# Four-part KANs on four column strips, and bank-emptying copies given out at the head of a turn

## The chip, the cores and the metric

The kernel runs on one core of a Trainium2 chip. A core has five engines that run side by side, each with a queue of its own that it works through in order: TensorE (PE in the profile; PEld is its loading of weights), VectorE (DVE), ScalarE (ACT), GpSimd (POOL) and SyncE (SP), which here only issues DMAs. TensorE writes its results into PSUM, eight banks of 128 x 512 float32, and ScalarE and VectorE copy them out. The metric is the time on the device in microseconds, lower is better: the median over several executions.

## The reference, cut to what matters

Sixteen sequences of 512 tokens with 128 channels pass through six residual steps, each on a layer-normed input:

```python
x = x + 0.5 * kan(ln(x))                 # L0_ffn
x = x + attention(ln(x))                 # L0_attn: 16 query heads and 4 key heads of 8, causal, rotary
x = x + 0.5 * kan(ln(x))                 # L0_ffn again, same weights
x = x + 0.5 * experts(ln(x))             # L1_ffn: 8 experts, each takes its top 128 tokens
x = x + recurrence(ln(x))                # L1_attn: a gated linear scan along the tokens
x = x + 0.5 * experts(ln(x))             # L1_ffn again

def kan(x, Win, bin_, W1, b1, W2, b2, Wout, bout):      # M = 64, INNER = 16
    s = jnp.einsum('btd,dm->btm', x, Win) + bin_
    h = jax.nn.relu(s[..., None] * W1 + b1)             # 64 x 16 = 1024 hidden values a token
    g = jnp.einsum('btmh,mh->btm', h, W2) + b2
    return jnp.einsum('btm,md->btd', g, Wout) + bout
```

A KAN is run 32 times, twice for each sequence. Its hidden layer has 1024 values for each token, which are eight tiles of 128 partitions x 512 tokens; what matters here is how the eight tiles are summed back to 64 channels.

## The kernel before, in words

The kernel has a front part (constants, first KANs), an attention part of 16 blocks, and an expert part.

**Blocks and turns.** Block b (0 to 15) has 44 turns. A turn gives out one step of `weights` for sequence b (the scores transposed into a bank `ps_st`, L622, then the exponential on ScalarE, L625, then the causal mask on GpSimd, L627) and one step of `maxima` for sequence b + 1 (the scores into a bank `ps_sc`, L564, and their row maximum on VectorE, L569 and L574). Both kinds of banks exist twice, so TensorE can be two turns ahead of ScalarE and of VectorE. Blocks -1 and 15 do only one of the two.

**Side work.** Everything else is written as Python generators that are advanced by one step in `turn()` (L1046): first those in `urgent`, then those in `sides`. The order in which a generator emits its instructions is the order in the engines' queues (TensorE, ScalarE, VectorE, GpSimd are ordered by hand; DMA issues on SyncE follow the program). Side work that needs a PSUM bank takes one of two shared banks with `bank()` (L222) and gives it back with `freed()` (L231). Typical is `turned` (L285): in one turn four transposes into a bank; in the next turn, after that turn's exponential and maximum have been emitted, the copy out of the bank. In blocks 0 to 15 the side work is paced: `need()` holds a step back when what it wants of an engine (in rough units) is over what is left of the turn's budget `MOST` (L197), and `take()` books work without waiting.

**A KAN** (`kan`, L299) norms and transposes x, multiplies by `win`, whose 64 columns stand in it twice, so that 128 partitions hold the 64 channels in two copies (L303), copies the result to `kan_s` (L307), and then in eight steps, paced to 15 turns, makes a hidden tile on ScalarE from `kan_s` with a scale and a bias for each partition (L329): a tile holds two of the 16 inner units of all 64 channels. After every second step two matmuls (L335) sum two hidden tiles into the bank `ps_kg`, the one into partitions 0 to 63, the other into 64 to 127; their weights `w2d` are 128 x 64, so the two stand on different column halves of the array. One copy (L340) and four matmuls with `wout` (L346) end it. `kan_held` lets one KAN at a time into this part.

**Attention's input** (`attn_in`, L375) makes queries and keys in float32 and cuts each into three bfloat16 parts in `parts` (L353): copy on ScalarE, subtract on GpSimd, copy on ScalarE, subtract on GpSimd. **Outputs** (`outputs`, L633) multiplies the weights with the values, four groups of heads on four column strips of 32 (L645), copies the bank (L651), transposes it (L656) and divides (L660, L661). The tail of `stage_out` runs a row's second KAN and its gate.

**The front part** issues the weights' DMAs on ScalarE's and SyncE's queues (L68, L123 to L157), and `prepare` (L466) makes the KAN's constants. **The expert part** (L1107) alternates one step of `experts` with one turn of side work (the recurrence, the routing, the transposes of gathered tokens).

Of the kernel before, what the change touches and what calls it, by code (L numbers as in the profile page):

```python
# [16 lines left out]
P = 128  # L17
S = 512
# [3 lines left out]
HALF = 8  # L22
# [22 lines left out]
def tile_macaron(  # L45
# [51 lines left out]
    with ExitStack() as ph:  # L97
# [5 lines left out]
        hp = ph.enter_context(tc.tile_pool(name="p1_h", bufs=4))  # L103
# [14 lines left out]
        win = cst.tile([D, 2, M], F32, name="win")  # L118
        binc = cst.tile([P, 1], F32, name="binc")
        kw1 = cst.tile([P, HALF], F32, name="kw1")  # L120
        kb1 = cst.tile([P, HALF], F32, name="kb1")
        kw2 = cst.tile([P, HALF], F32, name="kw2")
        nc.scalar.dma_start(out=win, in_=win_in.unsqueeze(1).to_broadcast([D, 2, M]))  # L123
        nc.scalar.dma_start(out=kw1, in_=kw1_in.rearrange("m (a h) -> a m h", a=2))
        nc.scalar.dma_start(out=binc, in_=bin_in.unsqueeze(0).to_broadcast([2, M]))
        nc.scalar.dma_start(out=kb1, in_=kb1_in.rearrange("m (a h) -> a m h", a=2))
        nc.scalar.dma_start(out=kw2, in_=kw2_in.rearrange("m (a h) -> a m h", a=2))
        kb2 = cst.tile([M, 1], F32, name="kb2")
        nc.scalar.dma_start(out=kb2, in_=kb2_in.unsqueeze(1))
        wout = cst.tile([P, D], F32, name="wout")  # L130
        nc.scalar.dma_start(out=wout, in_=wout_in.unsqueeze(0).to_broadcast([2, M, D]))
# [3 lines left out]
        rbias = cst.tile([P, HALF], F32, name="rbias")  # L135

        w2d = cst.tile([P, HALF, M], F32, name="w2d")
        eye2 = cst.tile([P, M], F32, name="eye2")
# [16 lines left out]
        nc.sync.dma_start(out=rope, in_=rope_in)  # L155
        for b in range(1, B):
            load(b)  # L157
# [75 lines left out]

        def together(*gs):

            got, live = [None] * len(gs), list(enumerate(gs))
            while live:
                left = []
                for i, g in live:
                    try:  # L240
                        next(g)
                        left.append((i, g))
                    except StopIteration as end:
                        got[i] = end.value
                live = left
                if live:
                    yield
            return got
# [36 lines left out]
        def turned(src, name, pool):  # L285
            ps = yield from bank([P, NT, P], F32, "ps_t", 0.55)
            for c in range(NT):
                nc.tensor.transpose(ps[:, c, :], src[:, c, :], ident)
            yield
            dst = pool.tile([P, S], F32, name=name)  # L290
            take(act=0.6)
            nc.scalar.copy(dst, ps.rearrange("p c q -> p (c q)"))
# [6 lines left out]
        def kan(b):  # L299

            _, xT = yield from norm(x[b])
            ps = yield from bank([P, S], F32, "ps_s", 0.9)
            nc.tensor.matmul(ps, lhsT=win.rearrange("d a m -> d (a m)"), rhs=xT, start=True, stop=True)  # L303
            yield
            sk = w2p.tile([P, S], F32, name="kan_s")
            take(act=0.6)
            nc.scalar.copy(sk, ps)  # L307
            freed()
            yield
            while kan_held[0]:  # L310
                yield
            kan_held[0] = 1
# [4 lines left out]
            for t in range(HALF + 1):  # L317
                while now[0] < begin + 15 * t // 8:
                    yield
                pair = t % 2 == 0 and t > 0  # L320
                work = {"act": 0.8} if t < HALF else {}
                if pair:
                    work["pe"] = 1.0
# [3 lines left out]
                if t < HALF:  # L327
                    h = hp.tile([P, S], F32, name="kan_h")
                    nc.scalar.activation(h, sk, AF.Relu, bias=rbias[:, t : t + 1], scale=kw1[:, t : t + 1])  # L329
                    hs.append(h)  # L330
                if t == 1:
                    nc.gpsimd.tensor_tensor(x[b], x[b], kcst.unsqueeze(1).to_broadcast([P, NT, D]), ALU.add)
                if pair:
                    for i in range(2):
                        nc.tensor.matmul(pg[i * M : (i + 1) * M, :], lhsT=w2d[:, t - 2 + i, :], rhs=hs[t - 2 + i],  # L335
                                         start=(t == 2), stop=(t == HALF))
                yield
            gT = hp.tile([P, S], F32, name="kan_h")
            take(act=0.6)
            nc.scalar.copy(gT, pg)  # L340
# [4 lines left out]
            for c in range(NT):  # L345
                nc.tensor.matmul(po[:, c, :], lhsT=gT[:, bass.ts(c, P)], rhs=wout, start=True, stop=True)  # L346
            yield
            take(dve=0.7)
            nc.vector.tensor_add(x[b], po, x[b])
# [3 lines left out]
        def parts(r, dst, copies, **work):  # L353
# [4 lines left out]
            yield from need(pool=1.15)  # L358
            nc.gpsimd.tensor_tensor(r, r, dst[:, 0, :], ALU.subtract)
            yield  # L360
            yield from need(**work)
            copies(dst[:, 1, :], r)
# [12 lines left out]
        def attn_in(b, st):  # L375
# [8 lines left out]
            nc.tensor.matmul(pa, lhsT=wq.rearrange("k h d -> k (h d)"), rhs=xT, start=True, stop=True)  # L384
            yield
            take(dve=0.7)
            nc.vector.tensor_mul(ta, pa, rope[:, 0, :])
            freed()
            pb = yield from bank([P, S], F32, "ps_pb", 0.9)
            nc.tensor.matmul(pb, lhsT=wqr.rearrange("k h d -> k (h d)"), rhs=xT, start=True, stop=True)  # L390
            yield
            take(dve=0.7)
            nc.vector.tensor_mul(tb, pb, rope[:, 1, :])
            freed()
            pk = yield from bank([2 * KR, S], F32, "ps_pk", 0.9)
            nc.tensor.matmul(pk, lhsT=wk.rearrange("k w h d -> k (w h d)"), rhs=xT, start=True, stop=True)
            yield
# [3 lines left out]
            nc.vector.tensor_mul(ka, pk[0:KR, :], rope[0:KR, 0, :])  # L401
            pv = yield from bank([P, NT, KR], F32, "ps_v", 0.9)
            for c in range(NT):
                nc.tensor.matmul(pv[:, c, :], lhsT=xT[:, bass.ts(c, P)], rhs=wv, start=True, stop=True)
            yield
            take(dve=0.7)
            nc.vector.tensor_mul(kb, pk[KR : 2 * KR, :], rope[KR : 2 * KR, 1, :])
# [3 lines left out]
            yield  # L411

            take(dve=0.3)
# [3 lines left out]
            nc.vector.tensor_copy(va[:, :, :, 0:HD], pv.rearrange("p c (r d) -> p c r d", d=HD))  # L417
# [3 lines left out]
            def keys():  # L421
                yield from need(pool=1.25)
                nc.gpsimd.tensor_tensor(ka, ka, kb, ALU.add)
                yield
# [27 lines left out]
        def center_win():  # L452
            psc = yield from bank([P, 2 * M], F32, "ps_kc0")
            centered(psc, win.rearrange("d a m -> d (a m)"))
            freed()
# [10 lines left out]
        def prepare():  # L466

            nc.vector.scalar_tensor_tensor(rbias, in0=kw1, scalar=binc, in1=kb1, op0=ALU.mult, op1=ALU.add)
            nc.vector.tensor_add(eye2, ident[:, 0:M], ident[:, M:P])
            for u in range(HALF):  # L470
                nc.vector.tensor_scalar(w2d[:, u, :], eye2, kw2[:, u : u + 1], 0.5, ALU.mult, ALU.mult)
# [5 lines left out]
            nc.tensor.matmul(psc, lhsT=kb2, rhs=wout[0:M, :], start=True, stop=True)  # L477
# [100 lines left out]
        def max_rows(b, half, maxs):  # L578
# [15 lines left out]
            for c in range(NT):  # L594
                nc.tensor.transpose(pm[:, c, :], ms[:, c, :, :].rearrange("p i h -> p (i h)"), identb)
            yield
            mr = w2p.tile([3 * H2, S], BF16, name="mr")
            take(dve=0.4)
            nc.vector.tensor_copy(mr, pm.rearrange("p c q -> p (c q)"))
# [33 lines left out]
        def outputs(b, st, r):  # L633
# [4 lines left out]
            for c in range(NT):  # L638
# [5 lines left out]
                for g in range(NG):  # L644
                    nc.tensor.matmul(po[32 * g : 32 * g + 32, c * P : S], lhsT=va[:, c, r, :],  # L645
                                     rhs=pt[:, g, OFF[c] : OFF[c] + n], start=(c == 0), stop=(c == NT - 1))
                if c in (0, NT - 1):
                    yield
            oT = w2p.tile([P, NT, P], F32, name="oT")
            yield from need(act=0.6)  # L650
            nc.scalar.copy(oT.rearrange("p c q -> p (c q)"), po)  # L651
# [3 lines left out]
            for c in range(NT):  # L655
                nc.tensor.transpose(pq[:, c, :, :].rearrange("p r w -> p (r w)"), oT[:, c, :], ident)  # L656
            yield
            rd = small.tile([P, NT, NG, 1], F32, name="rden")
            take(dve=0.55)
            nc.vector.reciprocal(rd, pq[:, :, :, HD : HD + 1])  # L660
            nc.vector.tensor_mul(y[:, :, r, :, :], pq[:, :, :, 0:HD], rd.to_broadcast([P, NT, NG, HD]))  # L661
# [4 lines left out]
        def stage_out(b, st):  # L666
# [4 lines left out]
            for c in range(NT):  # L671
                nc.tensor.matmul(po[:, c, :], lhsT=yT[:, bass.ts(c, P)], rhs=wo, start=True, stop=True)
            yield
            take(dve=0.7)
            nc.vector.tensor_add(x[b], po, x[b])
# [10 lines left out]
        def gated(k, b):  # L686
# [4 lines left out]
            for c in range(NT):  # L691
                nc.tensor.matmul(ps[:, c, :], lhsT=xT[:, bass.ts(c, P)], rhs=gateT, start=True, stop=True)
            yield
            take(dve=0.2)
            nc.vector.tensor_copy(scores[b // GB][:, :, b % GB, :], ps)
# [116 lines left out]
        def dispatch():  # L812
            while taken[0] < NR * B:
                yield
            for i in range(0, len(order), 2):
# [10 lines left out]
                for j in range(2):  # L826
                    nc.tensor.transpose(ps[:, j, :], xgs[i // E % 2][:, i % E + j, :], ident)
                yield
                copy = nc.vector.tensor_copy if i % 4 else nc.scalar.copy
                copy(xins[i // E % 2][:, i % E : i % E + 2, :], ps)  # L830
# [105 lines left out]
        def folded():  # L936


            tmp = w2p.tile([P, 2, M, 4], F32, name="wu", tag="kan_s")
# [41 lines left out]
        def recurrence(pair):  # L981
# [6 lines left out]
            for a in range(2):  # L988
                nc.tensor.matmul(pf[half[a], :], lhsT=wf, rhs=xTs[a], start=True, stop=True)
            yield  # L990
            fg = w2p.tile([P, S], F32, name="fg", tag="kan_s")
            nc.scalar.activation(fg, pf, AF.Tanh, scale=0.5)
# [5 lines left out]
            nc.tensor.matmul(pl, lhsT=wlam, rhs=fg, start=True, stop=True)  # L998
            yield
# [165 lines left out]
```

## Time and profile before

| | us |
|---|---|
| median of 3 executions | 1751.41 (1749.4 to 1756.8) |
| the profiled execution, its own time | 1746.91 |
| its span, first to last instruction | 1745.2 |
| TensorE busy in the span | 1636.9 (94%) |
| VectorE, ScalarE, GpSimd busy | 1107.3, 996.6, 977.6 |

The profile is one execution. A group row names line, engine, operation, the tiles written and read, the shape and the count, then the busy time in us, the mean ns of one, and the idle time of the engine before it. Ends of matmuls are modelled and overlap the next matmul's start, so that what a product costs TensorE is read from its start to the start of the next product in the timeline. The first score product of block 0 starts at 116.3 us, the blocks' first turns then at 161.7, 215.2, 276.5, 332.1, 387.6, 443.2, 498.8, 554.3, 609.9, 667.3, 721.5, 782.0, 841.5, 897.3 and 949.7, and the first expert product at 1003.0. Blocks 3 to 8 take 55.6 us each.

### The profile page before, as it was taken

What the parts mean: (1) busy time and instruction counts of PE and PEld (TensorE: products, weight loads), DVE (VectorE), ACT (ScalarE), POOL (GpSimd) and SP (SyncE); (2) the same over time, 40 slices, a digit from 0 to 9 for tenths busy, and PEclk for the clock granted to TensorE, in tenths of its full rate; (3) what the DMA queues carried; (4) which work ended last, traced back from release to release, by engine and by line L of the source; (5) the groups of instructions that cost most, each with busy time, mean ns of one, the idle gap of its engine ahead of it and who ended that gap; (6) DMA issues with size and microseconds to landing.
All of it is one profiled execution on the core that took longest, in us unless ns stands there. A gap on an engine that the chain in (4) does not pass through costs nothing. (4 is left out here: it accounts for less than half of the span.)

```text
span 1745.2 us, 35245 instructions
## 1 busy us (share of the span) xinstructions
PE 1636.9 (94%) x12879; PEld 1111.0 (64%) x12879; DVE 1107.3 (63%) x3604; ACT 996.6 (57%) x2000; POOL 977.6 (56%) x1453
## 2 busy tenths in 40 slices
PE   6788999999999999899899899999999999999997
PEld 2334444444444444444444389899988889989997
DVE  6677767777787788788876137643467444672222
ACT  3445667777777776677667654344443334444443
POOL 2524535545565455455534767567663777647773
PEclk9889999999999999999999899999998999999999
DMA  4211111011110111011122113233322233323342
GB/s 117 76 52 36 44 44 43 28 42 51 54 37 32 42 55 47 16 48 54 35 70 63 31 44 73 51 64 73 62 60 45 55 73 63 66 56 71 68 82 48
DMA packets 101753, 94.77 MB, mean 54 GB/s; under 512 B 11859, under 2 KB 90140, under 8 KB 101340
## 3 DMA queue, kind: packets, MB, share of 16 engines
q1 hardware_dynamic: 74512, 67.45, 12.5%
q0 software_dynamic: 26048, 24.93, 8.8%
q8 instruction: 101, 1.65, 0.4%
q14 instruction: 72, 0.59, 0.1%
q10 hardware_dynamic: 1020, 0.15, 0.0%
HBM read 58.93 MB, written 37.49 MB: 55 GB/s over the span
## 5 line engine op out<-in xcount | busy, mean ns | idle before, releaser
L625 ACT ACTIVATE pt<-ps_st 128x512 f32<-128x512 f32 (+1 forms) x704 | 386.9, 561 | 238.3 <-PE ps_st L622 232.9
L627 POOL TENSOR_SCALAR_AFFINE_SELECT pt<-pt 128x128 f32<-128x128 f32 (+2 forms) x704 | 247.0, 355 | 405.0 <-ACT pt L625 400.4
L569 DVE CUSTOM_DVE_ANT_0 below<-ps_sc,causal 128x512 bf16<-128x512 f32 (+1 forms) x512 | 316.5, 618 | 117.2 <-PE ps_sc L564 103.1
L881 ACT ACTIVATE mo<-ps_h 128x512 f32<-128x512 f32 x256 | 153.1, 598 | 262.2 <-PE ps_h L879 262.0
L805 POOL DMA_INDIRECT xg<-xnd,tokI x256 | 249.9, 976 | 80.5 <-issue 42.8
L879 PE MATMUL ps_h<-xin,mw 128*128 128x128 f32 x2048 | 281.1, 281 | 0.0
L894 PE MATMUL ps_y<-mw,mo 128*128 128x128 f32 x2048 | 274.7, 278 | 0.0
L564 PE MATMUL ps_sc<-kp,qp 72*128 72x512 bf16 (+3 forms) x1024 | 260.7, 307 | 10.6 <-DVE maxs L569 8.0
L622 PE MATMUL ps_st<-qp,kp 99*128 99x512 bf16 (+3 forms) x1024 | 259.8, 307 | 5.7 <-ACT pt L625 4.8
L879 PEld LDWEIGHTS ps_h<-xin,mw 128*128 128x128 f32 x2048 | 252.7, 194 | 6.3 <-issue 3.7
L926 POOL DMA_INDIRECT sum<-ye,tokI x124 | 201.3, 1624 | 97.7 <-ACT ye L897 31.2
L894 PEld LDWEIGHTS ps_y<-mw,mo 128*128 128x128 f32 x2048 | 251.7, 194 | 2.3 <-issue 1.0
L622 PEld LDWEIGHTS <-kp 99*128 99x128 bf16 x1024 | 94.2, 101 | 203.8 <-issue 185.4
L329 ACT ACTIVATE kan_h<-kan_s,rbias,kw 128x512 f32<-128x512 f32 x256 | 206.6, 814 | 7.1 <-PE ps_kg L335 6.9
L574 DVE TENSOR_REDUCE maxs<-ps_sc 128x2 f32<-128x512 f32 (+1 forms) x192 | 130.6, 685 | 70.5 <-PE ps_sc L564 69.3
L335 PE MATMUL ps_kg<-kan_h,w2d 128*64 128x512 f32 x512 | 164.7, 640 | 3.1 <-ACT kan_h L329 3.0
L645 PE MATMUL ps_av<-pt,va 128*32 128x512 f32 (+3 forms) x2048 | 166.8, 444 | 0.0
L564 PEld LDWEIGHTS <-qp 72*128 72x128 bf16 x1024 | 97.5, 100 | 55.6 <-issue 33.9
L900 DVE TENSOR_TENSOR mo<-mo 128x128 bf16<-128x128 f32 x132 | 38.3, 290 | 137.8 <-ACT mo L885 137.6
L912 PE MATMUL acc<-mo 128*128 128x128 bf16 x1584 | 113.0, 220 | 6.0 <-DVE mo L900 5.8
L912 PEld LDWEIGHTS <-mo 128*128 128x128 bf16 x1584 | 99.5, 99 | 23.8 <-issue 22.5
L645 PEld LDWEIGHTS ps_av<-pt,va 128*32 128x32 f32 x2048 | 53.6, 109 | 93.0 <-issue 49.7
(195 smaller groups left out, 2308.8 us busy)
## 6 DMA issues: line engine op xcount, KB each, us to landing
qp<-qs SPq DMA_DIRECT2D x64, 288.0 KB
xnd<-kan_x SPq DMA_DIRECT2D x32, 256.0 KB
sum<-x SPq DMA_DIRECT2D x31, 256.0 KB
qs<-qpart SPq DMA_DIRECT2D x48, 128.0 KB
kp<-ks SPq DMA_DIRECT2D x48, 96.0 KB
x<-in_L_attn_x_dram SPq DMA_DIRECT2D x16, 256.0 KB
mw<-in_L_ffn_w_dram SPq DMA_DIRECT2D x16, 256.0 KB
xg<-xnd,tokI POOLq DMA_INDIRECT x256, 2.5
```

Of the source, the lines that this page charges most:

```text
L329: nc.scalar.activation(h, sk, AF.Relu, bias=rbias[:, t : t + 1], scale=kw1[:, t : t + 1])
L564: nc.tensor.matmul(v[:, u, 0:n], lhsT=qp[r][0 : 9 * HD, g, bass.ts(c, P)], rhs=kp[0 : 9 * HD, r, 0:n], start=alone, stop=(u == len(gs) - 1 ...
L569: nc.vector.tensor_tensor_reduce(below[:, 0:n], v[:, 0, 0:n], causal[:, S - n : S], 1.0, LOWEST, ALU.add, ALU.max, accum_out=maxs[:, c, h ...
L622: nc.tensor.matmul(v[:, u, 0:n], lhsT=kp[ROWS, r, bass.ts(c, P)], rhs=qp[r][ROWS, g, c * P : S], start=True, stop=True)
L625: nc.scalar.activation(o, v[:, :, 0:n], AF.Exp, scale=HD ** -0.5)
L627: nc.gpsimd.affine_select(out=dg, in_=dg, compare_op=ALU.is_ge, fill=0.0, base=0, pattern=[[0, len(gs)], [1, P]], channel_multiplier=-1)
L645: nc.tensor.matmul(po[32 * g : 32 * g + 32, c * P : S], lhsT=va[:, c, r, :], rhs=pt[:, g, OFF[c] : OFF[c] + n], start=(c == 0), stop=(c == ...
L805: nc.gpsimd.indirect_dma_start(out=xgs[i // E % 2][:, i % E, :], out_offset=None, in_=xnd[b], in_offset=bass.IndirectOffsetOnAxis(ap=tokI[ ...
L879: nc.tensor.matmul(pst[:, f, :], lhsT=mw1[e][:, bass.ts(f, P)], rhs=xins[i // E % 2][:, i % E, :], start=True, stop=True)
L894: nc.tensor.matmul(py, lhsT=hs[u][:, f, :], rhs=mw2[e][:, f, :], start=(f == 0), stop=(f == NF - 1))
L912: nc.tensor.matmul(acc[:, c, :], lhsT=sels[u][:, bass.ts(c, P)], rhs=yes[u][:, w, :], start=(e == 0 and c == 0 and w == 0), stop=(e == las ...
L926: nc.gpsimd.indirect_dma_start(out=sums[k, b], out_offset=bass.IndirectOffsetOnAxis(ap=tokI[g][:, n : n + 1], axis=0), in_=ye[:, b % 2 * ( ...
```

## The change

- The KAN works in four parts instead of two copies. `win` holds each half of the 64 channels four times, and the product with it is made twice, once for each half (`ps_s`, then `kan_s0` and `kan_s1`). A hidden tile holds four inner units of 32 channels. The eight tiles are summed by two groups of four matmuls, each with 128 x 32 weights, each matmul on a column strip of its own (at steps 4 and 8, instead of pairs at steps 2, 4, 6 and 8). Hidden tiles have five buffers instead of four. The constants are laid out to match, with more and smaller DMAs, some of them moved from ScalarE's queue to SyncE's.
- Copies and other operations that empty a bank of side products are put on a list `later` when the product is given out, and `flush()` emits them at the head of the next turn, ahead of that turn's score products, exponential and maximum. Before, they came after these. The same call stands in the expert part ahead of the experts' step.
- In `parts`, the second bfloat16 part is made on GpSimd by a subtraction that writes bfloat16 (ScalarE copy before), so that the order is copy, subtract, subtract, subtract.
- The front runs 17 turns instead of 14 before the second sequence's input starts, the keys start two steps later, and `mr` has one buffer instead of two.

The diff, cut to its core (the other bank-emptying operations, L651 to L1023, are moved to `later` in the same way):

```diff
-HALF = 8
+MH = M // 2
+NI = 4
+NV = 4
...
+        win = cst.tile([D, 2, NI, MH], F32, name="win")
+        binc = cst.tile([P, 2], F32, name="binc")
+        kw1 = cst.tile([P, 2, NV], F32, name="kw1")
+        def inner(dst, src):
+            for half in range(2):
+                rows = src[half * MH : (half + 1) * MH, :]
+                nc.scalar.dma_start(out=dst[:, half, :], in_=rows.rearrange("m (i v) -> i m v", i=NI))
+        for half in range(2):
+            cols = win_in[:, half * MH : (half + 1) * MH]
+            nc.sync.dma_start(out=win[:, half, :, :], in_=cols.unsqueeze(1).to_broadcast([D, NI, MH]))
+        def out_weights():
+            for half in range(2):
+                rows = slice(half * M, half * M + MH)
+                nc.sync.dma_start(out=kb2[rows, :], in_=kb2_in[half * MH : (half + 1) * MH].unsqueeze(1))
+                nc.sync.dma_start(out=wout[half * M : (half + 1) * M, :],
+                                  in_=wout_in[half * MH : (half + 1) * MH, :].unsqueeze(0).to_broadcast([2, MH, D]))
...
         nc.sync.dma_start(out=rope, in_=rope_in)
+        out_weights()
         for b in range(1, B):
             load(b)
...
+        later = []
+        def flush():
+            for emit in later:
+                emit()
+            later.clear()
...
             for c in range(NT):
                 nc.tensor.transpose(ps[:, c, :], src[:, c, :], ident)
-            yield
             dst = pool.tile([P, S], F32, name=name)
+            later.append(lambda: nc.scalar.copy(dst, ps.rearrange("p c q -> p (c q)")))
+            yield
             take(act=0.6)
-            nc.scalar.copy(dst, ps.rearrange("p c q -> p (c q)"))
             freed()
...
-            ps = yield from bank([P, S], F32, "ps_s", 0.9)
-            nc.tensor.matmul(ps, lhsT=win.rearrange("d a m -> d (a m)"), rhs=xT, start=True, stop=True)
-            yield
-            sk = w2p.tile([P, S], F32, name="kan_s")
-            take(act=0.6)
-            nc.scalar.copy(sk, ps)
-            freed()
-            yield
-            while kan_held[0]:
-                yield
-            kan_held[0] = 1
+            sk = []
+            for half in range(2):
+                while half and kan_held[0]:
+                    yield
+                kan_held[0] |= half
+                ps = yield from bank([P, S], F32, "ps_s", 0.9)
+                nc.tensor.matmul(ps, lhsT=win[:, half, :, :].rearrange("d i m -> d (i m)"), rhs=xT,
+                                 start=True, stop=True)
+                sh = (w1p if half else w2p).tile([P, S], F32, name=f"kan_s{half}")
+                later.append(lambda sh=sh, ps=ps: nc.scalar.copy(sh, ps))
+                yield
+                take(act=0.6)
+                freed()
+                sk.append(sh)
+            yield
...
+            U = 2 * NV
+            for t in range(U + 1):
                 while now[0] < begin + 15 * t // 8:
                     yield
+                four = t in (U // 2, U)
+                work = {"act": 0.8} if t < U else {}
+                if four:
                     work["pe"] = 1.0
                 if t == 1:
                     work["pool"] = 1.25
                 yield from need(**work)
+                if four:
+                    for half, v, h in hs:
+                        o = half * M + v % 2 * MH
+                        nc.tensor.matmul(pg[o : o + MH, :], lhsT=w2d[:, half, v, :], rhs=h,
+                                         start=(t < U), stop=(t == U))
+                    hs = []
+                if t < U:
+                    half, v = t // 2 % 2, t // 4 * 2 + t % 2
                     h = hp.tile([P, S], F32, name="kan_h")
+                    nc.scalar.activation(h, sk[half], AF.Relu, bias=rbias[:, half, v : v + 1],
+                                         scale=kw1[:, half, v : v + 1])
+                    hs.append((half, v, h))
...
             copies(dst[:, 0, :], r)
             yield
             yield from need(pool=1.15)
+            nc.gpsimd.tensor_tensor(dst[:, 1, :], r, dst[:, 0, :], ALU.subtract)
+            yield
+            yield from need(pool=1.15)
             nc.gpsimd.tensor_tensor(r, r, dst[:, 0, :], ALU.subtract)
-            yield
-            yield from need(**work)
-            copies(dst[:, 1, :], r)
             yield
             yield from need(pool=1.3)
             nc.gpsimd.tensor_tensor(dst[:, 2, :], r, dst[:, 1, :], ALU.subtract)
...
-            yield from need(act=0.6)
-            nc.scalar.copy(oT.rearrange("p c q -> p (c q)"), po)
+                    later.append(lambda: nc.scalar.copy(oT.rearrange("p c q -> p (c q)"), po))
...
         def turn():
+            flush()
             urgent[:] = [g for g in urgent if step(g)]
             sides[:] = [g for g in sides if step(g)]
             refill()
...
             for i in range(TURNS):
+                flush()
                 step(wts)
                 step(mxs)
...
+        working = True
+        while working or sides:
+            flush()
+            working = step(main)
             turn()
```

## The prediction

> **What bounds the kernel now.** Read first: the page's busy shares, then engines by stretch (stretch, length, then busy time and count of PE, PEld, DVE, ACT, POOL, clock, DMA).
>
> ```profile
> PE 1636.9 (94%) x12879; PEld 1111.0 (64%) x12879; DVE 1107.3 (63%) x3604; ACT 996.6 (57%) x2000; POOL 977.6 (56%) x1453
> 443.20:498.80 55.60, 54.72 (x397) 26.90 (x397) 42.98 (x144) 42.03 (x77) 30.09 (x63) 1.00 0.13 43
> 721.50:782.00 60.50, 55.28 (x393) 27.59 (x392) 49.39 (x161) 41.38 (x76) 31.50 (x64) 0.97 0.12 40
> ```
>
> The second line is block 6, one of six alike: TensorE 98% busy, VectorE and ScalarE 76 to 77%. The third is a block with routing on VectorE (49.4 of 60.5). Busy alone proves little, as matmuls overlap; so next, TensorE's waits, first in blocks 4 to 8, then behind them:
>
> ```profile
> PE ps_s L303 <- ACT kan_xT L292: 3.6, 5, 0.7
> PE ps_o L672 <- ACT yT L292: 0.8, 5, 0.2
> ...
> PE ps_t L288 <- DVE y L661: 7.2, 5, 2.9
> PE ps_st L622 <- ACT pt L625: 3.0, 8, 0.5
> PE ps_ko L346 <- DVE rope_kb L407: 2.1, 1, 2.1
> ```
>
> Five blocks hold 4.4 us of waits. TensorE's stream sets the time there; later some waits on operations that empty side banks (L661, L407) come in. Then what a product costs, from TensorE's timeline of block 6 (start, length, engine and line), start to next start:
>
> ```profile
> 473.63 1.02 PE L303 MATMUL ps_s<-kan_xT,win 128*128 128x512 f32 x2
> 474.50 0.38 PE L622 MATMUL ps_st<-qp,kp 99*128 99x512 bf16 x1
> ...
> 481.20 2.02 PE L335 MATMUL ps_kg<-kan_h,w2d 128*64 128x512 f32 x4
> 483.15 0.39 PE L622 MATMUL ps_st<-qp,kp 99*128 99x256 bf16 x2
> ...
> 484.65 0.38 PE L564 MATMUL ps_sc<-kp,qp 72*128 72x512 bf16 x1
> 484.96 1.08 PE L335 MATMUL ps_kg<-kan_h,w2d 128*64 128x512 f32 x4
> 485.97 0.39 PE L622 MATMUL ps_st<-qp,kp 99*128 99x512 bf16 x1
> 486.20 0.38 PE L564 MATMUL ps_sc<-kp,qp 72*128 72x512 bf16 x1
> 486.51 1.06 PE L645 MATMUL ps_av<-pt,va 128*32 128x512 f32 x8
> 487.51 0.39 PE L622 MATMUL ps_st<-qp,kp 99*128 99x512 bf16 x1
> 487.73 0.38 PE L564 MATMUL ps_sc<-kp,qp 72*128 72x512 bf16 x1
> 487.95 0.38 PE L622 MATMUL ps_st<-qp,kp 99*128 99x512 bf16 x1
> ```
>
> The first product with `win` takes 0.87. A KAN pair takes 1.01 (484.96) when both hidden tiles are there, and 1.95 (481.20) when the second is late. Four strips of 128 x 32, each with its own 128x512 operand, take 1.00 (486.51): four matmuls for the price of two. A score product ahead of strips takes 0.31, elsewhere 0.22 (487.73): 0.09 for each entry.
>
> **The change, part by part.** The sum is against the profiled execution, 1746.91 us (span 1745.2 and 1.7 around it), 4.5 below the median of 1751.41.
>
> *Pairs to quads.* 26 KANs run in blocks 0 to 15. Their 104 pairs, added up in the timeline, hold TensorE 125.6 us, 4.83 a KAN; 4.05 of it would be four undisturbed pairs, 0.78 is lateness. After: two groups at 1.00, two entries fewer (-0.18), one product with `win` more (+0.87). That is 4.83 + 0.18 - 2.00 - 0.87 = 2.14 a KAN, 56 us; if all the lateness comes back elsewhere 1.36, 35 us. The lateness is ScalarE's backlog of hidden tiles. A group of four has its last tile given out two turns ahead, as a pair has, but meets it twice a KAN, not four times; on the other hand TensorE's turns without side products, 0.33 to 0.45 in the timeline, grow more frequent, and there the exponential (0.49 start to start) and a hidden tile (0.70) are what is waited for. I keep a third of 20: -42.
>
> The row of four strips decides this. The Trainium skill, TensorE: Matmul & The Clock Gate, Part 3, gives three column tiles side by side 2.38 times the speed of one, 0.79 for each. By that rule four would come to 3.2 times; with 0.97 for a matmul alone (half of the late pair) a group would take 3.9/3.2 = 1.2 us, an estimate, and 52 such groups would make the sum 11 us poorer. The trace does not agree: its group of the same shape took 1.00.
>
> *Routing blocks.* Blocks 9 to 13 have VectorE at 49.4 of 60.5. If TensorE's share falls by 4, VectorE's own work is 87% of the rest: some of the gain of these ten KANs (about 16) stays behind. From 0 to +15, near the low end as VectorE still has room: +5.
>
> *Second copy to `kan_s`.* 26 more copies on ScalarE (L307: 580 ns, 0.46 start to start), cover: ScalarE idles 13.6 us of block 6, two more copies take 1.2. In `parts` two casts a block leave it (L362, 617 ns), so its load stands. 0; without cover +12. The Trainium skill, TensorEngine Tiling, PSUM Bottleneck, warns that tiling doesn't speed up evacuation: by it this copy would count. ScalarE's 76% here lets it hide.
>
> *GpSimd's extra subtraction.* Two a block at 1.15 (the row of L359) on 30.1 of 55.6. Behind them on its queue stand the masks L627, whose readers are the value products two steps later. A row's input begins four blocks ahead and must be ready two blocks later, so a few turns more hold nobody: 0, up to +4. The `mr` copies with one buffer are half a block (28 us) apart, their DMAs keep their place: 0.
>
> *`flush`.* The copy moves ahead of the next turn's score evacuations on ScalarE and VectorE. Its product stands on TensorE ahead of those scores, so it is ready first and holds nobody idle. What stands behind it (exponential, maximum) comes 0.46 to 0.68 later; with two score banks TensorE feels that only over three light turns in a row. The bank comes free by one exponential or maximum sooner: of the waits shown (L661, L407, kan_xT; 13 us in blocks 4 to 15) I take a quarter: -3, from -8 to +10.
>
> *Front and tail.* Five KANs run before block 0 (0 to 116 us), latency-bound: one more product and copy each (0.87 + 0.58), three turns more. On SyncE's queue four issues stand newly ahead of `wq` and four ahead of the 15 loads of x, at the 0.4 to 0.5 that its issues take; they push the second row's load from 5.3 to about 9 us, and its norm starts at 22.5. ScalarE issues fewer. Against it stand the shorter sums: +2, from -4 to +8. In the experts the same TensorE stream is untouched, and gaps at `ps_x` and `acc` (about 10 us) can move either way: -1, from -4 to +3.
>
> Sum: -42 + 5 + 0 + 0 - 3 + 2 - 1 = **-39**: 1708 profiled, **1712** as a median. With the ends of the terms 1694 to 1728.
>
> **The rivals.** *Half of it stays behind* (chance 0.21): light turns are limited by ScalarE and VectorE in order; lateness returns in full (35 instead of 42), routing keeps 15, the copy isn't hidden for half its 12: -35 + 15 + 6 - 3 + 1 = -16, about 1735, from 1728 to 1742. For it: 3.0 us of waits `ps_st` on exponentials already in the late blocks; against: none in blocks 4 to 8.
>
> *Slower* (0.07, above 1760): copies at the head of the queue hold the exponentials and maxima back, and TensorE waits at `ps_st` and `ps_sc`. Some 30 such operations stand in a block, 480 in all; to use up the 39 and another 8.8 each has to cost TensorE 0.10 us. At 0.15 it is 72 - 39 = +33, 1784. Against it: in block 6 no three light turns follow one another, and the work is only exchanged within a turn.
>
> *No change* (0.06, 1743 to 1760): TensorE streams less, but waits as much more for exponentials and maxima, 2.4 us a block. That is the limit of which the half case is the middle: 1751. Against it: ScalarE's 42.0 and VectorE's 43.0 of 55.6 would have to grow to full queues.
>
> *More* (0.07, below 1694): all lateness goes (-56) and the late waits with it (-8): 1746.9 - 64 + 4.5 + 3 = 1690.
>
> **How the numbers follow.** The forecast, 1694 to 1728, has 0.59. With the half case (0.21) and part of the one below, the range 1689 to 1743 holds 0.84. About 0.5% (8.8 us) can be told from no change: faster 0.87 (0.59 + 0.21 + 0.07), same 0.06, slower 0.07.
>
> **What would show it.** Right: group rows of L335 with 128*32 forms, from start to next start 1.0 for eight; blocks 3 to 8 at 51 to 52 us; TensorE's waits there still few; twice as many copies to `kan_s`. Wrong: groups of four that start one after the other (a late tile); waits of `ps_st` on L625 or `ps_sc` on L569 over 1 us a block; a front later than 120 us; more turns at blocks' ends.

## The result and the profile after

| | before | after |
|---|---|---|
| median, us | 1751.39 | 1711.22 (1703.04 to 1714.79) |
| ratio | 1 | 0.9766, 95% interval 0.9747 to 0.9785 |
| span of the profiled execution | 1745.2 | 1713.1 (its own time 1714.79, the longest of four) |
| front, to the first score product of block 0 | 116.3 | 120.7 |
| attention part, 16 blocks | 880.1 | 840.6 |
| of it blocks 0-2, 3-8, 9-15 | 160.2, 333.4, 386.5 | 151.0, 323.1, 366.5 |
| block 15's end to the first expert product | 6.6 | 10.0 |
| from there to the end | 742.1 | 741.7 |

The forecast of 1712 held. The gain lies in the attention part: it gave 39.5 us between the two profiles, while the front and the stretch behind block 15 lost 7.8 (the profiled executions differ by 32.1, the medians by 40.2). A second profile of the kernel after gave 117.5 and 842.0 for its front and attention part. But the gain is not spread as forecast: blocks 3 to 8 gave 1.7 us each instead of about 4, and blocks 9 to 15 gave 20.0, where the forecast's terms come to some 16 (an estimate: 11 of the 26 KANs at a share of 42 us, less the 5 for routing, and the 3 of the order).

The page's busy shares of the kernel after:

```profile
PE 1593.3 (93%) x12943; PEld 1106.1 (65%) x12943; DVE 1124.4 (66%) x3606; ACT 1000.5 (58%) x2000; POOL 1019.0 (59%) x1486
```

Its block 6 and a block with routing by engine (length, then busy time and count of PE, PEld, DVE, ACT, POOL, then clock and DMA). VectorE is at 83% in the first, ScalarE at 79%:

```profile
433.30:487.00 53.70, 51.41 (x400) 26.31 (x399) 44.71 (x142) 42.29 (x77) 32.98 (x64) 1.00 0.14 45
708.10:763.50 55.40, 53.08 (x400) 26.91 (x399) 48.35 (x160) 42.14 (x78) 32.12 (x65) 1.00 0.13 43
```

TensorE's timeline in block 6 of the kernel after:

```profile
468.45 1.06 PE L365 MATMUL ps_kg<-kan_h,w2d 128*32 128x512 f32 x8
469.45 0.34 PE L669 MATMUL ps_st<-qp,kp 99*128 99x384 bf16 x1
469.62 0.33 PE L611 MATMUL ps_sc<-kp,qp 72*128 72x384 bf16 x1
469.79 1.02 PE L338 MATMUL ps_s<-kan_xT,win 128*128 128x512 f32 x2
470.65 0.33 PE L669 MATMUL ps_st<-qp,kp 99*128 99x384 bf16 x1
```

A group of four takes 1.00 from start to next start, and this product with `win` 0.86, as forecast; over blocks 3 to 8 the products with `win` take 1.00 on average, as a wait that follows one counts to it. All 24 groups of blocks 3 to 8 take 1.00: the lateness is gone from them. But TensorE now waits for others. Its waits, first in blocks 4 to 8 and then behind them:

```profile
PE ps_st L669 <- ACT pt L672: 4.6, 10, 0.6
PE ps_m L642 <- DVE ms L637: 2.5, 5, 0.5
PE ps_t L318 <- DVE y L709: 2.1, 5, 0.4
PE ps_t L318 <- DVE kan_x L308: 1.0, 5, 0.2
...
PE ps_st L669 <- ACT pt L672: 12.0, 30, 0.7
PE ps_t L318 <- DVE kan_x L308: 4.3, 3, 3.5
PE ps_t L318 <- DVE y L709: 3.2, 4, 1.2
...
PE ps_ko L386 <- DVE rope_kb L445: 0.8, 1, 0.8
```

In blocks 4 to 8 waits rose from 4.4 us to 10.2, and the score products hide more of them: adding up each product's time to the next start, the stream of blocks 3 to 8 (before, after) holds KAN groups 58.0, 24.0; `win` 10.9, 24.1; score products 133.9, 144.7; the rest 130.6, 130.3. The KAN gave 20.8 us, and the scores took 10.8 back. In blocks 9 to 15 the KAN gave 17.0, the rest 4.6, and the scores took 1.6. There the waits for `y` and `rope_kb` became less (7.2 to 3.2 and 2.1 to 0.8), those for exponentials more (3.0 to 12.0). The mean granted clock of blocks 11, 13 and 14 rose from 0.97 to 1.00. Block 10 alone became slower, from 54.2 to 58.6 us (57.0 in the second profile).

### The profile page after: what moved, and what is told of

Same layout as the page of the kernel before. It is cut to its first block, busy times and chain, and to the rows that moved or that the text cites. A ratio compares the mean times of both kernels' runs of the same rounds, so it can differ in the third digit from the quotient of the medians.

```text
span 1713.1 us, 35403 instructions
## 1 busy us (share of the span) xinstructions
PE 1593.3 (93%) x12943; PEld 1106.1 (65%) x12943; DVE 1124.4 (66%) x3606; ACT 1000.5 (58%) x2000; POOL 1019.0 (59%) x1486
## 5 line engine op out<-in xcount | busy, mean ns | idle before, releaser
L674 POOL TENSOR_SCALAR_AFFINE_SELECT pt<-pt 128x128 f32<-128x128 f32 (+2 forms) x704 | 251.7, 364 | 333.2 <-ACT pt L672 328.2
L672 ACT ACTIVATE pt<-ps_st 128x512 f32<-128x512 f32 (+1 forms) x704 | 378.6, 563 | 100.6 <-PE ps_st L669 94.7
L978 POOL DMA_INDIRECT sum<-ye,tokI x124 | 200.3, 1616 | 94.4 <-issue 38.1
L294 POOL TENSOR_TENSOR ln_rstd<-ln_rstd,mhalf 128x4 f32<-128x4 f32 x96 | 101.7, 1059 | 8.0
```

Source lines behind the costliest of these rows:

```text
L672: nc.scalar.activation(o, v[:, :, 0:n], AF.Exp, scale=HD ** -0.5)
L674: nc.gpsimd.affine_select(out=dg, in_=dg, compare_op=ALU.is_ge, fill=0.0, base=0, pattern=[[0, len(gs)], [1, P]], channel_multiplier=-1)
L978: nc.gpsimd.indirect_dma_start(out=sums[k, b], out_offset=bass.IndirectOffsetOnAxis(ap=tokI[g][:, n : n + 1], axis=0), in_=ye[:, b % 2 * ( ...
```

## The experiments

Two readings had to be told apart: "stream" (the forecast: the groups of four give nearly all, the order of the copies about 3 us) and "order" (the order gives half). The attention part is the measure that all profiles share: from the first score product of block 0 to block 15's last turn (0.8 us after that turn's start), read from the timeline. On the chip of four of the runs (marked *) the expert part took 814 to 830 us instead of 733 to 742 and the kernel before 1839 us, so their totals are read as ratios to it alone. No kernel was profiled both on that chip and on another. That attention parts can be compared across them is argued: the kernel before is 88 us slower there in total and the expert part alone 72 to 88, and an exponential of 128x512 takes 598 to 601 ns in all these profiles.

| kernel | ratio to before | attention part | 0-2 | 3-8 | 9-15 |
|---|---|---|---|---|---|
| before | 1 | 880.1 | 160.2 | 333.4 | 386.5 |
| after, second profile | 0.9761 [0.9738, 0.9783] | 842.0 | 151.8 | 323.1 | 367.1 |
| order alone * | 0.9859 [0.9784, 0.9934] | 865.0 | 156.8 | 335.9 | 372.3 |
| all but the order * | 1.0177 [1.0118, 1.0236] | 899.5 | 157.8 | 344.7 | 397.0 |
| after, ScalarE's alone ahead * | 0.9899 [0.9864, 0.9933] | 871.9 | 154.6 | 332.2 | 385.0 |
| after, VectorE's alone ahead * | 0.9874 [0.9804, 0.9943] | 859.1 | 151.3 | 329.9 | 377.9 |
| half the hidden tiles | 0.9750 [0.9732, 0.9768] | 840.8 | 151.7 | 322.9 | 366.1 |
| second part cast on ScalarE | 0.9807 [0.9791, 0.9824] | 846.2 | 156.5 | 328.8 | 361.0 |
| second `kan_s` copy on VectorE | 0.9777 [0.9749, 0.9806] | 843.7 | 150.9 | 323.3 | 369.5 |
| half the maxima's keys | 1688.09 us, one run | 822.4 | 153.0 | 313.2 | 356.1 |
| both halved | 1673.75 us, one run | 812.1 | 146.8 | 312.0 | 353.3 |
| outputs from turn 12 | 0.9696 [0.9672, 0.9720] | 824.7 | 145.6 | 320.1 | 359.0 |
| input from turn 34 | 0.9789 [0.9768, 0.9811] | 839.5 | 148.5 | 329.7 | 361.4 |

**The kernel after once more**, as the measure for the others.

> The kernel after, unchanged, beside the others of this call, since the chip of the four runs before it gave the kernel before 1839 us instead of 1751, with the attention part at its usual length. Both theories: the attention part (first turn of block 0 to the last turn of block 15) is 840.6 us as in its first profile, within 3; whatever the chip adds lies behind 961 us.

842.0 against 840.6: from this one pair, attention parts can be compared from run to run within some 2 us. Each of blocks 3 to 8 repeats to 0.1 us.

**The order alone, and all but the order.** The first is the kernel before with every bank-emptying operation put on `later` (and one buffer for `mr`); the second is the kernel after with these lines taken out, so that `turn()` emits them behind the scores' exponential and maximum:

```diff
             for i in range(TURNS):
-                flush()
                 step(wts)
                 step(mxs)
...
-            flush()
             step(mxs)
...
         while working or sides:
-            flush()
             working = step(main)
```

> The kernel before with the bank-emptying operations ahead of the next turn's exponential and maxima; KANs stay in pairs, parts and front as before. Theory 'stream' (the prediction's terms: quads give nearly all, the order gives 3): 1748, between 1743 and 1761; blocks 3 to 8 stay at 55.6 us, blocks 9 to 15 near 386. Rival 'order' (half of the 40 us comes from the order, since blocks 9 to 15 gained 20.0 us in the profile and blocks 3 to 8 only 10.3): 1728 to 1738, with blocks 9 to 15 near 370 and VectorE's waits at rope_kb and y gone.

> The kernel after with the bank-emptying operations given out behind the turn's exponential and maxima again, and all the rest of the change in place. Theory 'stream': 1711 to 1718, blocks 3 to 8 at 53 to 54 us. Rival 'order': 1725 to 1735, blocks 9 to 15 back to 380 or more. A third reading, that the order costs in blocks 3 to 8 (ScalarE waits 24 us for ps_av and ps_t at the queue's head there): blocks 3 to 8 fall to 52 us and the whole is at or below the kernel after.

The order alone gave 15.1 us of attention: 3.4 in blocks 0 to 2 and 14.2 in 9 to 15, which is near what "order" expected there (though the waits for `y` fell only from 7.2 to 5.1), while blocks 3 to 8 lost 2.5. Some 5 us of it go with the clock (an estimate: in blocks 11, 13 and 14, 168.8 us before, its mean rose from 0.97 to 1.00). All but the order is slower than before: +19.4, and +11.3 of it in blocks 3 to 8; neither reading had that. The parts don't add: -15.1 and +19.4 make +4.3, and together they gave -39.5 (-38.1 in the second profile). Put otherwise, all the rest of the change costs 19.4 us without the order and gives 23.0 on top of it (865.0 to 842.0, on two chips). TensorE's waits in blocks 4 to 7 of the kernel without the order:

```profile
PE ps_s L338 <- ACT kan_s L341: 3.3, 4, 0.8
PE ps_t L318 <- DVE y L709: 2.9, 4, 0.7
PE ps_m L642 <- DVE ms L637: 2.7, 4, 0.7
PE ps_oq L704 <- ACT kan_xT L320: 2.2, 4, 0.6
```

A stretch of its block 5 and the rest of that block (columns as above):

```profile
404.90:415.70 10.80, 8.67 (x47) 5.15 (x45) 5.44 (x16) 5.97 (x12) 4.75 (x8) 0.84 0.17 60
415.70:453.40 37.70, 36.24 (x280) 17.29 (x280) 29.69 (x107) 31.26 (x57) 20.23 (x45) 1.00 0.12 39
```

And TensorE's timeline in the first of them:

```profile
406.29 0.66 PE L704 MATMUL ps_oq<-ident,oT 128*128 128x128 f32 x4 [0.56 <-ACT kan_xT L320]
...
409.09 0.63 PE L318 MATMUL ps_t<-ident,y 128*128 128x128 f32 x4 [0.73 <-DVE y L709]
...
411.11 2.01 PE L338 MATMUL ps_s<-kan_xT,win 128*128 128x512 f32 x2 [0.83 <-ACT kan_s L341]
```

The side products stand in line for the two shared banks, and each waits for a copy that stands behind an exponential or a maximum. ScalarE's timeline shows it for the last of the three:

```profile
409.98 0.60 ACT L672 ACTIVATE pt<-ps_st 128x512 f32<-128x512 f32 x1 [1.68 <-PE ps_st L669]
410.47 0.58 ACT L341 COPY kan_s<-ps_s 128x512 f32<-128x512 f32 x1
```

The exponential waits for its scores on TensorE, the copy stands behind the exponential, and TensorE's next product with `win` waits for the copy. The three waits fall within 6 us, and the granted clock drops in this stretch (0.84 on average): the second product with `win` takes 1.80 to the next start instead of 0.86. Blocks 3 to 5 have this drop and take 58.2 us, blocks 6 to 8 don't and take 56.6, with the same three waits to 0.01 us. Block 6 at the same place:

```profile
463.42:474.20 10.78, 8.66 (x57) 4.74 (x56) 6.71 (x20) 6.78 (x13) 5.83 (x10) 1.00 0.21 67
469.35 1.12 PE L338 MATMUL ps_s<-kan_xT,win 128*128 128x512 f32 x2 [0.83 <-ACT kan_s L341]
```

So without the order a block takes 1.0 us more than before, and where the clock drops another 1.6; what decides whether it drops stays open. In block 6 of the kernel after, the same place has one wait of 0.42 and the product takes 0.86. The kernel without the order still has the other small parts of the change; that it is the bank waits and not one of these that makes it slower than before is read from the waits, and from the next two runs.

**Whose operations.** `later` is split by engine, and one of the lists is emitted ahead, the other behind.

> The kernel after, with ScalarE's bank-emptying operations alone ahead and VectorE's behind the maxima. 'Stream': within 4 us of the kernel after, 1709 to 1716. 'Order', if it is VectorE's operations that matter (their waits stood in the late blocks before): 1720 to 1730, most of it in blocks 9 to 15.

> The kernel after, with VectorE's bank-emptying operations alone ahead and ScalarE's behind the exponential. 'Stream': within 4 us of the kernel after. 'Order': also within 4 us, as VectorE's are those that matter; if ScalarE's matter as much, 1718 to 1726. If ScalarE's copies at the head of the queue are what slows blocks 3 to 8, these fall below 53.9 us.

Against 899.5 with none ahead, ScalarE's alone give 27.6 us, VectorE's alone 40.4, both 57.5. That VectorE's alone would be within 4 us of the kernel after, as both readings had it, was wrong by 17 (by the ratios, 0.9874 against 0.9761). That fits two banks that go round, where a late copy of either engine holds the next side product.

**What limits blocks 3 to 8.** The scores' 10.8 us could come from ScalarE. Its hidden tiles were halved, which leaves the hidden layer of half the tokens out:

```diff
-                    nc.scalar.activation(h, sk[half], AF.Relu, bias=rbias[:, half, v : v + 1],
+                    nc.scalar.activation(h[:, 0 : S // 2], sk[half][:, 0 : S // 2], AF.Relu, bias=rbias[:, half, v : v + 1],
...
-                        nc.tensor.matmul(pg[o : o + MH, :], lhsT=w2d[:, half, v, :], rhs=h,
+                        nc.tensor.matmul(pg[o : o + MH, :], lhsT=w2d[:, half, v, :],
+                                         rhs=h[:, 0 : S // 2].unsqueeze(1).to_broadcast([P, 2, S // 2]),
```

> The kernel after, each hidden tile made for 256 of the 512 tokens only (about 0.3 us less on ScalarE for each of 256 instructions); the sums read those columns twice, so TensorE's work is the same. It leaves the hidden layer of half the tokens out. Theory 'TensorE streams': blocks 3 to 8 stay at 53.9 us within 0.5. Rival 'ScalarE sets the pace in the light turns' (score products cost 144.7 us in blocks 3 to 8 against 133.9 before, as they wait for exponentials): 51 to 52 us a block, 35 us less in all 16.

No change: a tile fell from 804 ns to 591 (medians of blocks 3 to 8), ScalarE's busy time in a block by 3 us, and the blocks stayed at 53.9. TensorE's waits in blocks 4 to 8 show where it went:

```profile
PE ps_m L643 <- DVE ms L638: 2.5, 5, 0.5
PE ps_t L318 <- DVE y L710: 2.1, 5, 0.4
PE ps_st L670 <- ACT pt L673: 1.7, 5, 0.3
PE ps_sc L612 <- DVE maxs L617: 1.6, 5, 0.3
```

The waits for exponentials fell from 4.6 to 1.7, and waits for maxima, 1.6, are new: VectorE is as late as ScalarE, in the same turns. VectorE's timeline in the kernel after there, 4.5 us without a gap:

```profile
453.57 0.67 DVE L616 CUSTOM_DVE_ANT_0 below<-ps_sc,causal 128x512 bf16<-128x512 f32 x1
454.17 0.08 DVE L616 DVE_READ_ACCUMULATOR2_ANT maxs<- 128x1 f32 x1
454.17 0.37 DVE L291 BATCH_NORM_AGGREGATE ln_mv<-ln_st 128x2 f32<-128x6 f32 x4
454.48 0.56 DVE L616 CUSTOM_DVE_ANT_0 below<-ps_sc,causal 128x384 bf16<-128x384 f32 x1
454.96 0.08 DVE L616 DVE_READ_ACCUMULATOR2_ANT maxs<- 128x1 f32 x1
454.96 1.03 DVE L304 TENSOR_SCALAR kan_x<-x,ln_mv,ln_rstd 128x128 f32<-128x128 f32 x2
455.91 0.55 DVE L616 CUSTOM_DVE_ANT_0 below<-ps_sc,causal 128x384 bf16<-128x384 f32 x1
456.38 0.08 DVE L616 DVE_READ_ACCUMULATOR2_ANT maxs<- 128x1 f32 x1
456.38 0.59 DVE L304 TENSOR_SCALAR kan_x<-x,ln_mv,ln_rstd 128x128 f32<-128x128 f32 x2
456.90 0.55 DVE L616 CUSTOM_DVE_ANT_0 below<-ps_sc,causal 128x384 bf16<-128x384 f32 x1
457.37 0.08 DVE L616 DVE_READ_ACCUMULATOR2_ANT maxs<- 128x1 f32 x1
457.37 0.68 DVE L308 TENSOR_TENSOR kan_x<-x,ln_rstd 128x512 f32<-128x512 f32 x1
```

L304 and L308 belong to two norms, that of a row's gate and that of the second KAN of the row after it, in the same four turns. So VectorE was relieved, alone and together with ScalarE: the maxima of the wide tiles read half their keys.

```diff
-                                below[:, 0:n], v[:, 0, 0:n], causal[:, S - n : S], 1.0, LOWEST,
+                                below[:, 0 : n // 2], v[:, 0, 0 : n // 2], causal[:, S - n : S - n // 2], 1.0, LOWEST,
```

> The kernel after, with the row maxima of the 512- and 384-wide tiles taken over the first half of their keys only (VectorE has about 0.2 us less in each of 32 operations a block; the softmax is then scaled by a maximum over part of its row). With the hidden tiles halved the blocks 3 to 8 stayed at 53.9 us and a wait moved from ScalarE to VectorE's maxima. 'VectorE sets the pace': 51 to 52.5 us a block. 'Both do, in turn': 53.0 to 53.9, as ScalarE takes over. 'TensorE streams': 53.9.

> Half the hidden tiles' tokens and half the maxima's keys left out at once, TensorE's work as in the kernel after. 'Both engines limit the light turns in turn': blocks 3 to 8 fall to 51.5 us or less, though each alone did little. 'TensorE streams': still above 53.4. By the forecast's terms (55.6 less 4.3) 51.3.

With VectorE relieved blocks 3 to 8 fall to 52.2 us, with both to 52.0, and the late blocks by 11.0 and 13.8. TensorE's waits in blocks 4 to 8, first with VectorE relieved and then with both:

```profile
PE ps_st L669 <- ACT pt L672: 4.6, 10, 0.6
PE ps_t L318 <- DVE kan_x L308: 2.3, 5, 0.5
...
PE ps_t L318 <- DVE kan_x L308: 2.3, 5, 0.5
PE ps_st L670 <- ACT pt L673: 1.7, 5, 0.3
```

The waits for exponentials stay at 4.6 with VectorE relieved, and the blocks fall all the same; taking 2.9 of them out as well gives only 1.0 us over these five blocks. VectorE set the pace of the light turns, and "both in turn" was wrong, too. The two reliefs are not of one size: in block 6 VectorE's busy time fell from 44.7 us to 36.4, ScalarE's from 42.3 to 39.1. At 52.0 TensorE's waits in blocks 4 to 8 are 4.0 us; what is left is its stream, 0.7 above the 51.3 of the forecast's terms. Two smaller edits move work between the engines:

> The kernel after with the copy to the second half of kan_s on VectorE (two copies a block moved, 0.46 each on ScalarE, 0.6 on VectorE). 'TensorE streams': no change. 'ScalarE sets the pace': 0.5 to 1 us less a block in blocks 3 to 8, and in the routing blocks 9 to 13 no gain or a loss, since VectorE has 47 to 48 us of work in 55 there.

> The kernel after with the second bfloat16 part cast on ScalarE again, in the old order of the parts (two casts of 0.62 more a block on ScalarE, two subtractions of 1.15 fewer on GpSimd). 'TensorE streams': no change in the attention part, within 3 us. 'ScalarE sets the pace': 0.5 to 1.2 us more a block, 8 to 19 us in all.

The second copy to `kan_s` on VectorE (in `kan`, `nc.vector.tensor_copy` for the second half) changed blocks 3 to 8 by 0.2 us and cost 2.4 in the late ones, about as much as two runs differ. VectorE's busy time in block 6 rose from 44.7 to 46.6 at no cost, which speaks for where its work falls as the limit, and against its sum. The cast on ScalarE (the old `parts`) cost 5.7 us in blocks 3 to 8 and 4.7 in blocks 0 to 2, and gave 6.1 in the late ones: 4.2 in all. 0.95 us in each of blocks 3 to 8 is what "ScalarE sets the pace" expected (0.5 to 1.2), and doesn't fit the reading above by itself; VectorE's busy time in block 6 rose as well, to 46.3 with the same 142 operations. Which side of this edit it is, an engine's load or the order of the steps, was not separated.

**Moving the two norms apart.** A row's outputs begin four turns later, or, in the other kernel, a later row's input four turns sooner:

```diff
-IN, OUT = 38, 8
+IN, OUT = 38, 12
...
-IN, OUT = 38, 8
+IN, OUT = 34, 8
```

> The kernel after with a row's outputs begun in turn 12 of the next block instead of 8, so that the norm of its gate falls into other turns than the norm of the next row's first KAN (both stand in turns 16 to 19 of blocks 3 to 8, where TensorE waits about 2 us). If these waits come from two norms side by side: 0.5 to 1.5 us less a block, 1695 to 1706 beside a kernel after of 1706. If the waits only move: 1703 to 1712.

> The kernel after with a later row's input begun in turn 34 instead of 38: the same two norms four turns apart, the other way round. Norms side by side: 1695 to 1706. Waits that only move: 1703 to 1712.

The outputs from turn 12 give 1691.58 us (1690.12 to 1695.75), ratio 0.9696: faster than the kernel before and, with intervals that don't touch, than the kernel after, and below both expected ranges. Blocks 3 to 8 gain 0.5 us each, blocks 0 to 2 and 9 to 15 6.2 and 8.1. The input from turn 34 makes blocks 3 to 8 lose 6.6 us and the others gain 9.0; its ratio can't be told from that of the kernel after. The two norms in block 6, first with the outputs from turn 12 (the block starts at 423.75) and then with the input from turn 34 (433.29):

```profile
445.66 0.60 DVE L304 TENSOR_SCALAR kan_x<-x,ln_mv,ln_rstd 128x128 f32<-128x128 f32 x2
455.52 0.69 DVE L308 TENSOR_TENSOR kan_x<-x,ln_rstd 128x512 f32<-128x512 f32 x1
...
453.81 1.19 DVE L304 TENSOR_SCALAR kan_x<-x,ln_mv,ln_rstd 128x128 f32<-128x128 f32 x2
458.73 0.94 DVE L308 TENSOR_TENSOR kan_x<-x,ln_rstd 128x512 f32<-128x512 f32 x1
```

In the kernel after, whose block 6 starts at 433.31, they start 21.6 and 24.1 us into the block. The outputs from turn 12 move the KAN's norm alone, to 31.8 us, and leave the gate's at 21.9. The input from turn 34 moves another norm, that of a later row's first KAN, and leaves these two at 20.5 and 25.4, so it is no test of them. The one test left is borne out by 0.5 us a block; of the 14.3 us in the other blocks a part goes with the granted clock, whose mean rose from 0.91 to 1.00 in block 2 and from 0.86 to 1.00 in block 15. That the two norms were the cause stays argued.

## Why the prediction was right, point by point

*What bounds the kernel*: right for the kernel before. In the kernel after VectorE holds the six blocks 1.9 us above TensorE's stream, at which they stand with both other engines relieved (52.0).

*Pairs to quads, -42*: right in its place. Over all blocks the groups fell from 127.7 us (106 pairs; the prediction counted 104 and 125.6) to 60.2 and the products with `win` rose from 25.2 to 52.8: -39.9. The same shape's price, 1.00, held, so the estimate of 1.2 from the Trainium skill (TensorE: Matmul & The Clock Gate, Part 3) did not. But the saving is not free to take: without the order the same edit is 19.4 us slower, and on top of it the rest of the change gave 23.0. "I keep a third of 20" failed too: the lateness of the pairs in blocks 3 to 8 was 9.5 us (58.0 less 48 pairs at 1.01), and the scores there took 10.8 back, more than all of it.

*`flush`, -3, from -8 to +10*: this step failed. "Of the waits shown I take a quarter" counted the waits that the pairs' stream left, and took the two parts as independent. Alone it gave -15.1, more than all the waits that were counted (13 us), in part through the granted clock, which the term left out; with the rest of the change it decides over 57.5 us.

*Routing blocks, +5*: nothing stayed behind. Blocks 9 to 13 gave 16.5 us, all of the "about 16", with VectorE busy for 87% of block 11 (48.35 of 55.40), as forecast. Its work there was taken as a bound on TensorE; what counted more was the place of the bank-emptying operations of both engines. Moving them alone gave 9.6 us in these five blocks.

*Light turns*: the forecast had them cost two thirds of the lateness and named exponentials and hidden tiles, which are ScalarE's; blocks 3 to 8 took 53.9 instead of 51 to 52, and it was VectorE. The rival "half of it stays behind", which names both engines, comes nearest for these six blocks. Two of the forecast's own signs of being wrong showed: waits of `ps_st` on exponentials of 1.7 us a block in blocks 9 to 15 (12.0 in all), and a front of 120.7 in the first profile.

*Second copy to `kan_s`, 0*: right, the copy on the other engine changes nothing; the warning of the Trainium skill (TensorEngine Tiling, PSUM Bottleneck) that evacuation doesn't become faster applied elsewhere, to when banks come free. *GpSimd's extra subtraction, 0 up to +4*: with the order of steps that goes with it, it was worth 4.2 us as a gain. *Front +2, tail -1*: +4.4 and +3.0 in the first profile (10.0 less 6.6, and 0.4 gained in the expert part), +1.2 and -1.7 in the second; the front stood between 116.5 and 123.2 in the kernels that share it.

*Slower, 0.10 us an operation*: hardly. With the order alone blocks 3 to 8 lost 0.4 us each, with 6.1 us of waits for maxima that the kernel before doesn't have there: about 0.01 us for each of 30 operations.

*The range*: 1694 to 1728 is narrower than what the ends of the terms add up to, -72 to +5 without an unhidden copy, which is 1679 to 1756.

So the total came out by luck, by two errors of opposite sign and like size: the order alone gave 15.1 us where 3 was forecast, and the rest of the change on top of it 23.0 where 36 was.

## What to carry to other kernels

Where side products share few PSUM banks, the place of the copies in the engines' queues and the length of the products are one change: cutting TensorE's work first made this kernel slower, as the copies didn't move along. Price a reordering against the stream as it will be, not against the waits that the slower stream shows. When TensorE's gain is missing, relieve the other engines one at a time and then together: a wait that is named at one engine can hide another that is just as late.

## What the runs showed that was not expected

The same short waits can go with a drop of the clock or not: three of 0.56, 0.73 and 0.83 us within 6 us stood beside a mean granted clock of 0.84 over 10.8 us in blocks 3 to 5 of one kernel, and of 1.00 in its blocks 6 to 8. The expert part took 814 to 830 us on one chip and 733 to 742 on others, in kernels that differ there at most in the order of copies; the unchanged kernel before was 88 us slower in total on that chip.
